# Two convolution blocks: pairs of units in the scan stage, inlaid convolution blocks at other places, and three steps in another order

## The chip, the cores and the metric

The kernel runs on one core of a Trainium2 chip. A core has five engines that work through queues of their own and meet only at semaphores: TensorE (PE, with its weight loads shown apart as PEld), VectorE (DVE), ScalarE (ACT), GpSimd (POOL) and SyncE (SP, which here only issues transfers). TensorE writes to eight banks of PSUM, each of 128 partitions by 512 float32 values; the other operands lie in SBUF. The metric is the device time of one execution in microseconds. It is the median of several executions, and lower is better.

## The reference

The input x has the shape (8, 96, 96, 192) in float32. Two blocks follow each other, each with a group norm before it and a residual around it:

```
x = x + L0(gn(x));  x = x + L1(gn(x))        # gn: 32 groups of 6 channels, over the whole image

L0: proj  = gn(x) @ W_in + b_in              # 192 -> 384 channels
    local = depthwise 3x3 conv(proj)
    mixed = 0.25*(lr + rl + tb + bt) + local # four running means s = 0.6*s + 0.4*x: along w
                                             # forward and backward, along h forward and backward
    out   = layernorm(mixed) @ W_out + b_out # 384 -> 192

L1: y   = depthwise 7x7 conv(gn(x)) + bias
    y   = layernorm(y) @ w0 + b0             # 192 -> 768
    out = (gelu(y) @ w1 + b1) * gamma        # 768 -> 192
```

## The kernel before

The kernel has five stages in a row, with DRAM tensors between them. Nearly all of it stands in manual schedules: each engine works in the order in which the Python code emits its instructions, and a planner has no part in it. Pools of buffers add waits where a buffer comes round again.

**Stage A** (to about 756 us) computes the statistics of the first group norm and `proj`, which it stores by channel in `P_d`.

**Stage B** (to about 1793 us) is the stage of the scans. Of the 384 channels it takes four at a time, 96 blocks `k`, each as `NI` = 3 units `i`; one unit holds 128 rows (four sets of 32 values of w) by 2 x 4 images x 96 values of h. The loop (L779 to L827) runs over n = 3k + i, 291 passes, of which the last three only mix. One pass of it emits

- `conv_b` (L681): 24 products from `band` and `pin` into two PSUM tiles `pl` (pool `ps_l`, four banks), on TensorE as tiles of 34 rows by 32 columns. Each float32 product appears as two records, so a unit is 48 records at L688. Two ACT copies take the result into `loc` (L697), two more take the rows of one channel into `last` (L700).
- `scan_down` on VectorE (L721, along h downward), with a small POOL operation on its ends (L725), and `scan_up` of the unit before (L730).
- up to two store issues of finished results on POOL (L744).
- `mix_b` (L703) of the unit three passes earlier: eight products (16 records, L709 and L712, 128 or 96 rows by 32 columns) do the scans along w as a product with the matrices `mix` and `down`. They go into two PSUM tiles `pa` (pool `ps_a`, two banks), and ACT copies each to `mo` (L713).
- `add` (L775) on POOL, which adds z to `mo`.

On TensorE this gives convolution, mix, convolution, mix. Inputs `pin` and `band` are loaded through SP three blocks ahead.

**Stage C** (to about 2580 us) runs over 192 units u: TensorE turns and projects a column (`turn_c`, `project_c`, L1135 and L1141) into `pos` banks (pool `ps_o`, four banks, two for each unit), ACT sums squares (`square_c`, L1162), and in the next pass `scale_c` makes `ve` on VectorE (L1168) and `rs` on POOL (L1170), and `finish_c` on VectorE (L1175) scales and adds the residual into `x1c`, which frees the banks. `steps` holds lists of `bn_stats`, three at a time, which collect the statistics of the second group norm; after the first half of the images it also holds the five steps of `norm_c` (L980), each as a list of one: means, squares, powers, shift, spread. Two of them, squares and powers, begin with a product (`total`, L992) that stands in TensorE's queue behind the unit of the pass; powers and shift pass through a power on POOL (L1020). A pass takes its list from `steps` ahead of `finish_c`.

**Stage D** (to about 2902 us) is the first part of the 7x7 convolution. There are 32 blocks n (2 halves of the images x 16 sets of 12 channels); it does n = 0 to `N1` - 1 = 18. A block has 24 scalings of `raw` to `xin` (`scale_steps`, in three tiles t of eight, L958 on ACT for some n, L960 on VectorE) and a copy of `band` (`spread`, L964), then six `conv_d` (L1323): 12 products each (24 records at L1337, 63 rows by 64 columns) into two PSUM banks, and two ACT operations into `yo` (L1347). `bank` hands out the eight banks in a ring. `store_d` stores `yo` through SP. The results are loaded again as tiles `ya` and `yb` by `load_y`: `y_0` is tile 0, `y_1` tile 1, whose pieces go to SP or POOL; the last eight pieces of a tile (L1404) are on POOL. The layer norm of a unit of stage E is a chain of seven steps (`norm_steps_e`): sums, mean, center (VectorE), square (ACT, L1501), squares (VectorE), powers (POOL, L1513), scale (VectorE). The chain of the first two units runs during the last two blocks, n = 17 and 18: sums, mean, center of unit 0 ahead of block 17, and after the third `conv_d` of block 18 square, squares and powers of unit 0, sums, mean and center of unit 1, and scale of unit 0. The loads of `y_1` come at the end of block 17.

**Stage E** runs over 72 units u (a tile of y has two). A unit has a first layer in 3 parts for u < 36 and 2 parts later (`first_layer`: products of 128 rows, L1549, then of 64 rows, L1559; a gelu on ACT, L1568), and four `second_layer` of the unit before (L1579), with `xo` on VectorE (L1590) and a store on POOL (L1598). `turn_in` transposes the unit to come (L1534). Into the first units the 13 blocks left of the 7x7 convolution are laid: `slots` holds for each block three lists of scalings (on ACT) and six `conv_d` (in the pool `ps_y`, two banks), and `slot()`, called five times in a unit, takes the next list whatever it is. The five places are after the first part of the first layer and after each of the four second layers.

## Time and profile before

| what | value |
|---|---|
| time, median of 3 runs | 5424.39 us (5416.11 to 5430.3) |
| the profiled execution | 5428.47 us, its span 5426.5 us |
| granted clock of TensorE, mean | 0.986 |
| PE, DVE, ACT, POOL busy | 97%, 64%, 48%, 44% |
| stage A, 0 to 756: PE busy | 706.8 us |
| stage B, 756 to 1793: PE busy | 1029.1 of 1037 us |
| stage C, 1793 to 2580: PE busy | 765.3 of 787 us |
| stage D, 2580 to 2902: PE busy | 258.4 of 322 us, DMA share 0.97 |
| joint of D and E, 2902 to 2975: PE busy | 46.1 of 73 us |
| stage E with inlaid blocks, 2975 to 3880: PE busy | 901.2 of 905 us |
| stage E, rest: PE busy | 1540.7 of 1546 us |

The profile is that of one execution. A line in order of time has the start in us from the span's start, the duration of the group, the engine, the line of the code, the operation, what it writes and reads, the shape of the tile in TensorE's array (34*32 is 34 rows by 32 columns), the size and the number of records, and in brackets how long the engine was idle before it and what ended that. Records of a group may overlap, so the distance from start to start says more than the duration.

### The profile page before, as it was taken

The numbers are of one execution on the slowest core, as the hardware profiler recorded it, in microseconds if no ns is written. First come the engines' busy times: TensorE is split into PE (matmuls) and PEld (weight loads), VectorE is DVE, ScalarE is ACT, GpSimd is POOL, SyncE is SP. The second block draws the span as 40 slices with busy tenths as digits, with TensorE's granted clock in tenths as the row PEclk, the third lists the DMA queues.
The fourth block names the chain that finished last, engine by engine and source line by source line (L and its number), as shares of the span: only waits on it lengthen the run. The fifth ranks groups of instructions, "written<-read, shape, count | busy, mean of one in ns | idle before, by whom it ended". The sixth has DMA issues, their size and how long they took to land. (4 is left out here: it accounts for less than half of the span.)

```text
span 5426.5 us, 107918 instructions
## 1 busy us (share of the span) xinstructions
PE 5247.6 (97%) x42206; PEld 3346.3 (62%) x42206; DVE 3455.9 (64%) x6722; ACT 2581.9 (48%) x5765; POOL 2405.4 (44%) x2129
## 2 busy tenths in 40 slices
PE   6999999999999999999787999999999999999999
PEld 4666643333333799999454666666666666666667
DVE  6555539999999555555556555555566666566654
ACT  2444447777777566565434444454433333323232
POOL 1111128888888555555335222233233333333332
PEclk9999989999999999999898999999999999999999
DMA  7999869999999799899998455545433233332331
GB/s 221 285 286 277 251 183 239 247 240 244 246 243 246 230 306 308 273 301 312 282 308 206 119 137 135 131 120 138 108 79 78 80 81 85 87 92 80 81 78 41
DMA packets 784651, 1015.33 MB, mean 187 GB/s; under 512 B 322359, under 2 KB 658432, under 8 KB 782096
## 3 DMA queue, kind: packets, MB, share of 16 engines
q1 hardware_dynamic: 671432, 633.30, 44.3%
q0 software_dynamic: 86896, 336.90, 18.9%
q10 hardware_dynamic: 25816, 38.25, 3.1%
q8 instruction: 334, 5.47, 0.4%
q14 instruction: 173, 1.42, 0.1%
HBM read 603.70 MB, written 420.03 MB: 189 GB/s over the span
## 5 line engine op out<-in xcount | busy, mean ns | idle before, releaser
L1579 PEld LDWEIGHTS hp<-w1g,g 128*128 128x128 f32 x6912 | 1117.9, 190 | 140.7 <-issue 78.3
L1579 PE MATMUL hp<-w1g,g 128*128 128x192 f32 x6912 | 1174.9, 329 | 0.0
L1568 ACT ACTIVATE g<-hp,b0g 128x512 f32<-128x512 f32 x864 | 519.8, 693 | 1214.8 <-PE hp L1559 1191.9
L1598 POOL DMA_DIRECT2D out_dram<-xo x288 | 211.6, 735 | 1536.8 <-DVE xo L1590 1496.9
L1590 DVE TENSOR_TENSOR xo<-hp,r 128x384 f32<-128x384 f32 x288 | 229.0, 795 | 1002.2 <-PE hp L1579 998.7
L1549 PE MATMUL hp<-yT,w0w 128*128 128x512 f32 x1728 | 779.2, 597 | 22.1 <-DVE yT L1534 21.9
L1141 PE MATMUL po<-wc,mt 128*128 128x193 f32 x3456 | 667.4, 329 | 7.4 <-DVE x1c L1175 7.3
L688 PE MATMUL pl<-pin,band 34*32 34x380 f32 (+1 forms) x13824 | 636.6, 494 | 9.6 <-DMA pin<-PL_d 4.0
L775 POOL TENSOR_TENSOR mo<-mo,z 128x768 f32<-128x768 f32 x285 | 594.6, 2086 | 4.8 <-ACT mo L713 0.6
L1141 PEld LDWEIGHTS po<-wc,mt 128*128 128x128 f32 x3456 | 556.8, 192 | 9.0 <-DVE x1c L1175 8.6
L1549 PEld LDWEIGHTS hp<-yT,w0w 128*128 128x128 f32 x1728 | 321.2, 190 | 382.3 <-issue 350.5
L721 DVE TENSOR_TENSOR_SCAN z<-decay,loc 128x768 f32<-128x768 f32 x288 | 505.9, 1757 | 61.6 <-ACT loc L697 33.0
L730 DVE TENSOR_TENSOR_SCAN z<-decay,z 128x768 f32<-128x768 f32 x288 | 498.4, 1731 | 0.1
L1337 PE MATMUL hp<-xin,band 63*64 63x372 f32 (+1 forms) x4608 | 412.7, 496 | 70.9 <-ACT yo L1347 26.9
L688 PEld LDWEIGHTS pl<-pin,band 34*32 34x32 f32 x13824 | 234.4, 108 | 393.4 <-issue 386.7
L709 PE MATMUL pa<-loc,mix 128*32 128x384 f32 x3456 | 436.5, 498 | 0.0
L712 PE MATMUL pa<-last,down 96*32 96x384 f32 x1152 | 431.4, 498 | 1.0 <-ACT mo L713 1.0
L1559 PE MATMUL hp<-yT,w0w 64*128 64x512 f32 x1728 | 419.5, 611 | 0.0
L1513 POOL TENSOR_TENSOR rs<-tot,neg_half 32x32 f32<-32x32 f32 x72 | 395.6, 5494 | 46.1 <-DVE tot L1511 45.3
L1347 ACT ACTIVATE yo<-hp,dwb 128x384 f32<-128x384 f32 x384 | 197.1, 585 | 423.4 <-PE hp L1337 290.2
L697 ACT COPY loc<-pl 128x384 f32<-128x384 f32 x576 | 248.2, 483 | 312.3 <-PE pl L688 312.3
L395 PE MATMUL pm<-xT,win 128*128 128x384 f32 x1152 | 392.2, 491 | 0.0
(159 smaller groups left out, 7276.0 us busy)
## 6 DMA issues: line engine op xcount, KB each, us to landing
P<-po POOLq DMA_DIRECT2D x96, 1152.0 KB, 9.7
pin<-P SPq DMA_DIRECT2D x190, 576.0 KB
mt<-M SPq DMA_DIRECT2D x192, 384.0 KB
xq<-in_x_dram SPq DMA_DIRECT2D x96, 576.0 KB
xr<-in_x_dram SPq DMA_DIRECT2D x192, 288.0 KB
X<-x1c SPq DMA_DIRECT2D x144, 384.0 KB
out_dram<-xo POOLq DMA_DIRECT2D x288, 192.0 KB, 2.4
r<-X SPq DMA_DIRECT2D x35, 1536.0 KB
```

Of the source, the lines that this page charges most:

```text
L688: nc.tensor.matmul(pls[g][at * RB : (at + 1) * RB, :, lo:hi], band[rows, c, kh, :], pin[rows, c, :, NJ - 1 - j, lo + kh - 1 : hi + kh - 1] ...
L709: nc.tensor.matmul(pa[at], mix[:, i, at], loc[:, q], start=True, stop=True)
L712: nc.tensor.matmul(pa[at], down[:, to], last[:, q], start=True, stop=True)
L721: nc.vector.tensor_tensor_scan(zf, decay_f, loc.rearrange("p q n -> p (q n)"), 0.0, ALU.mult, ALU.add)
L730: nc.vector.tensor_tensor_scan(zr, decay_f, zr, 0.0, ALU.mult, ALU.add)
L775: eng.tensor_tensor(m, m, z, ALU.add)
L1141: nc.tensor.matmul(po, mt[:, m, j * 128 : (j + 1) * 128], wc[:, m], start=(m == 0), stop=(m == NC - 1),)
L1337: nc.tensor.matmul(pys[g][k * 64 : (k + 1) * 64, :, lo:hi], band[rows, k * GS + c, d * ZS : d * ZS + 64], xin[rows, :, :, k * GS + c, lo + ...
L1549: nc.tensor.matmul(hps[m, q], w0w[:, 0, m * 128 : (m + 1) * 128], yT[:, 2 * q], start=True, stop=False,)
L1559: nc.tensor.matmul(hps[m, q], w0w[p, 1, m * 128 : (m + 1) * 128], yT[p, 1], start=False, stop=True,)
L1568: nc.scalar.activation(g[:, m, q], hps[m, q], AF.Gelu, bias=b0g[:, m : m + 1], scale=1.0)
L1579: nc.tensor.matmul(po[:, q], g[:, m, q, k * 128 : (k + 1) * 128], w1g[:, m], start=(m == 0), stop=(m == NE - 1),)
```

## The change

In stage B the pass is cut into `begin_b` (the convolution's products), `local_b` (copy to `loc`, both scans), `keep_b` (copy to `last`) and `mixed_b` (stores, mix, add), and the loop takes two passes at a time. TensorE's order is then convolution n, convolution n + 1, mix n, mix n + 1. The order on ACT, VectorE and POOL stays: `loc`, `last`, `mo` of one pass, then of the next.

In stage C a list of a single step (those of `norm_c`) is run after `finish_c` of the pass, not before.

In stage D the third tile of block 18 is scaled on ACT, between the evictions of block 17; the copy of `band` and the first steps of unit 0's chain move up on VectorE accordingly. In block 18 the steps that stood after the third `conv_d` stand ahead of the first. The last eight pieces of `y_1` are issued after block 18, so behind the power of unit 0 on POOL. The `raw` loads of block 19 come after the load of `r` on POOL's queue.

In stage E each slot has a kind, `rows` or `conv`, and a place takes only its kinds: conv behind each of the three parts of the first layer, rows behind the second layers, both at the third second layer. The first layer has three parts as long as there are slots. In all 65 of the 78 inlaid `conv_d` stand between the 64-row products of the first layer and a second layer (15 before), 13 between a second and a first layer (63 between a second layer and a first or second layer before), and the first layer is cut into three parts in 28 units (36 before).

```diff
+            def local():
+                loc = wp.tile([128, NG, GB * S], F32, tag="loc", name="loc")
...
+            def keep():
+                at = slice(i * RB, (i + 1) * RB)
...
+            return local, keep
...
-                    locs[k, i] = conv_b(band, pin, i, lasts[k])
+                    halves[n] = conv_b(*now_b, i, lasts[k])
+            def local_b(n):
...
+                    locs[k, i] = halves[n][0]()
                     z = zs[k, i] = scan_down(locs[k, i])
...
-                if up_next is not None:
-                    scan_up(up_next)
-                up_next = z
+                if ups:
+                    scan_up(ups.pop(0))
+                if z is not None:
+                    ups.append(z)
+            def mixed_b(n):
...
+            for n in range(0, n_b, 2):
+                begin_b(n)
+                local_b(n)
+                keep_b(n)
+                if n + 1 < n_b:
+                    begin_b(n + 1)
+                    mixed_b(n)
+                    local_b(n + 1)
+                    keep_b(n + 1)
+                    mixed_b(n + 1)
+                else:
+                    mixed_b(n)
...
-            if n == 1 or n >= N1:
+            if n == 1 or n >= N1 or (n == N1 - 1 and t == NT - 1):
                 nc.scalar.activation(to, of, AF.Identity, bias=sh, scale=sc)
...
-                if steps:
-                    for step in steps.pop(0):
+                now = steps.pop(0) if steps else []
+                if len(now) > 1:
+                    for step in now:
                         step()
                 if held is not None:
                     ...
+                if len(now) == 1:
+                    now[0]()
...
-                NI + 1: y_1,
+                NI + 1: y_1[:-8],
...
                 if n == NI + 1:
                     chain = norm_steps_e(0)
-                    steps += chain[:3]
+                    per_t = len(steps) // NT
+                    between = steps[-1 - per_t : -1]
+                    steps = steps[: -1 - per_t] + steps[-1:] + chain[:3]
                     chain = chain[3:]
                 elif n == NI + 2:
                     nxt = norm_steps_e(1)
-                    between = chain[:3] + nxt[:3] + chain[3:]
-                    last = nxt[3:4]
+                    steps = chain[:3] + nxt[:3] + chain[3:]
+                    last = y_1[-8:] + nxt[3:4]
...
-                    if c == 2:
-                        for step in between:
-                            step()
+                    for step in between[2 * c : 2 * c + 2]:
+                        step()
...
-            for t in range(NT - 1):
-                load_raw(N1, t)
...
-        load_raw(N1, NT - 1)
...
         load_r(0, nc.gpsimd)
+        for t in range(NT):
+            load_raw(N1, t)
...
-            early_half = u < n_u // 2
-            parts, pool = (3, ps_h) if early_half else (2, None)
+            inlaid = bool(slots)
+            parts, pool = (3, ps_h) if inlaid else (2, None)
...
             first_layer(u, 0, parts, pool)
             chain.pop(0)()
-            slot()
+            slot("conv")
...
-            slot()
-            if early_half:
+            slot("rows")
+            if inlaid:
                 first_layer(u, 1, parts, pool)
+                slot("conv")
...
-            slot()
+            slot("rows", "conv")
...
-            if early_half:
+            if inlaid:
                 first_layer(u, 2, parts, pool)
+                slot("conv")
```

## The prediction

> **What bounds the kernel now.** I read the page first (TensorE busy 97%), then busy time by stage, because an average over stages with different limits says little; then the order of time inside the stretches that the change touches.
>
> The busy time of each engine in four stretches (span of the stretch, then busy time and instructions of PE, weight load, DVE, ACT, POOL; granted clock, DMA share, GB/s):
>
> ```profile
> 1300.00:1500.00 200.00, 200.00 (x3656) 69.13 (x3648) 193.93 (x115) 141.94 (x342) 175.04 (x190) 1.00 0.92 241
> 2240.00:2280.00 40.00, 32.69 (x200) 31.14 (x199) 15.72 (x46) 17.42 (x63) 20.89 (x16) 0.91 0.60 182
> 2900.00:2950.00 50.00, 27.95 (x102) 11.44 (x95) 39.62 (x87) 21.67 (x30) 20.87 (x14) 0.80 0.79 199
> 3200.00:3400.00 200.00, 200.00 (x1112) 123.79 (x1110) 102.90 (x213) 96.47 (x170) 61.33 (x30) 1.00 0.53 132
> ```
>
> Stage B (first row) has TensorE full, VectorE at 97% and the DMA engines at 92%: a gain on TensorE may run into one of them. The second row (the statistics inside stage C) and the third (from D to E) have holes in TensorE; the fourth, E with conv blocks in it, has none.
>
> One unit of stage B, in order of time (start, duration):
>
> ```profile
> 1400.32 2.15 PE L688 MATMUL pl<-pin,band 34*32 34x384 f32 x48
> ...
> 1402.40 0.52 PE L709 MATMUL pa<-loc,mix 128*32 128x384 f32 x2
> ...
> 1402.56 0.86 ACT L697 COPY loc<-pl 128x384 f32<-128x384 f32 x2 [0.89 <-PE pl L688]
> ...
> 1403.45 1.76 DVE L721 TENSOR_TENSOR_SCAN z<-decay,loc 128x768 f32<-128x768 f32 x1
> ...
> 1403.83 2.15 PE L688 MATMUL pl<-pin,band 34*32 34x384 f32 x48
> ```
>
> Convolution to mix 2.08 us, mix to the next convolution 1.43: the period is 3.51. A VectorE scan begins just as the copy of loc ends (1402.56 + 0.86), so TensorE sets the pace.
>
> **Part 1, two units at a time.** TensorE's order C M C M becomes C C M M; ACT, DVE and POOL keep their order. What goes is one pair of changes between array shapes (34x32 and 128x32) in two units. Six rounds of the convolution come to 6 x 0.3175 = 1.905 (at the start of B four convolutions run with no mix between, at half clock, and their loc copies start 3.81 apart: 1.905 at full clock) and four rounds of the mix to 1.27; 3.51 less 3.175 leaves 0.335 for a pair of changes. [...] Here two mixes now follow each other with two `pa` banks, which ACT must empty. The trace of before has such mixes, the last three of the stage:
>
> ```profile
> 1794.46 0.51 PE L712 MATMUL pa<-last,down 96*32 96x384 f32 x1 [0.95 <-ACT mo L713]
> ...
> 1795.38 0.48 ACT L713 COPY mo<-pa 128x384 f32<-128x384 f32 x1 [0.59 <-PE pa L709]
> ...
> 1795.91 0.51 PE L712 MATMUL pa<-last,down 96*32 96x384 f32 x1
> ```
>
> Start to start 1.45 (the next again 1.46), not 1.27: the second mix waits for the copy of the first, which ends at 1795.86. So a pair is 1.92 (C to C) + 2.08 (C to M) + 1.455 (M to M) + 1.43 (M to C) = 6.885, against 7.02: 0.135 saved. Regular units run from 816 to 1791 us: 975 / 3.51 = 278, 139 pairs, **19 us**; by the drain rule alone 47. The first six units end in a wait for input (789.6) that swallows their gain; nothing for them.
>
> Do the others keep up at 3.44? DVE: the second scan starts 1.67 to 1.68 after the first (1403.45 to 1405.12), 1.73 at most after the other: 3.34 to 3.41. The loc copies now come 3.8 and 3.1 apart, as loc(n+1) stands on ACT behind the copies of mix(n); six buffers let DVE run late by that 0.4. POOL is busy 3.07 a unit; the ends of scan n are fixed there more than 2 us before the upward scan needs them. The DMA share rises to 0.94. Bounds: 0 (one of them takes it all) to 47.
>
> **Part 2, the statistics behind finish_c** (stage C):
>
> ```profile
> 2249.00 1.82 PE L1141 MATMUL po<-wc,mt 128*128 128x193 f32 x6 [3.32 <-DVE x1c L1175]
> ...
> 2262.26 1.44 PE L1141 MATMUL po<-wc,mt 128*128 128x193 f32 x6 [2.26 <-DVE x1c L1175]
> ```
>
> DVE waits in a statistics step for a product queued behind a whole unit, with finish_c behind it, and TensorE then lacks a bank: 7.3 us with two more waits of 0.73 and 0.99, and some 3.7 more at half clock (200 instructions in 40 us where neighbouring stretches have 276: 11.0 in all). After: finish_c goes first. What is late next is the following unit's `ve`: in the squares step by gm to the reduction, 2.7 us, of which a unit of 3.9 hides all but 0.6. In the powers step POOL's power (5.44) still stands before `rs`: total to the freed bank stays 7.87 (2254.39 to 2262.26), less a unit of 3.9, 0.3 for the total and 0.4 of transposes leaves 3.2. So 7.3 becomes 3.8: **3.5 us**; the half clock may go or come with the 3.2 (bounds 0 and 8).
>
> **Part 3, from D to E.** In time, POOL's issues and TensorE's two long waits:
>
> ```profile
> 2909.05 2.28 POOL L1404 DMA_DIRECT2D yb<-Y  x4 [17.67 <-DMA yb<-Y]
> 2911.40 6.21 POOL L1513 TENSOR_TENSOR rs<-tot,neg_half 32x32 f32<-32x32 f32 x1
> ```
>
> ```profile
> 2922.37 5.23 PE L1549 MATMUL hp<-yT,w0w 128*128 128x512 f32 x8 [20.35 <-DVE yT L1534]
> ...
> 2970.67 4.04 PE L1337 MATMUL hp<-xin,band 63*64 63x384 f32 x24 [4.86 <-DVE band L964]
> ```
>
> The first power is ready at 2905.6 but sits behind four loads of `yb`, which wait. Ahead of it lie sums (bound by the landing of yb at 2890.3, not moved), center (ends 2896.4), ACT's square. After: square goes before block 18's evictions (2896.4 to 2899.4; before it ended at 2902.2), the DVE reduction and totals take 3.3 (2902.7), the power runs at once (to 2909) beside unit 1's sums to center (7.9 on DVE, to 2910.6), and the scale with transposes takes the same 4.73 to the first product: 2915.3, **7.1 us** sooner. What moves besides: block 18's evictions start 3 us later on ACT, and its last two convolutions wait for banks to about 2904, under the hole; eight scales of 0.45 go from DVE to ACT between evictions, where it idles 0.84 before each pair; y_1's eight POOL issues (0.57 each) now stand behind the power and land by about 2918, where sums of unit 2 want them at 2920.5 (a miss costs 2 to 3); six raw loads (0.62 each) go behind the 1.2 us issue of r on POOL's queue, so r lands earlier than 2947.9, and with it bias, the next power and DVE's band copy, which the second wait is for. The first conv slot also comes one product later. I take the **4.9** as gone: 12 us (bounds 2 and 18).
>
> **Part 4, conv blocks behind half-height products.**
>
> ```profile
> 3222.71 4.17 PE L1579 MATMUL hp<-w1g,g 128*128 128x192 f32 x24
> 3226.81 2.13 PE L1337 MATMUL hp<-xin,band 63*64 63x384 f32 x24
> 3228.86 3.70 PE L1549 MATMUL hp<-yT,w0w 128*128 128x512 f32 x8
> 3232.50 1.99 PE L1559 MATMUL hp<-yT,w0w 64*128 64x512 f32 x8
> 3234.41 2.13 PE L1337 MATMUL hp<-xin,band 63*64 63x384 f32 x24
> 3236.47 4.17 PE L1579 MATMUL hp<-w1g,g 128*128 128x192 f32 x24
> ```
>
> Between second and first layer a block costs 4.10 + 2.05 + 3.64 = 9.79, where without it the two take 4.00 + 3.53 (3245.92, 3253.82 and 3257.35 start such a run: 7.90 is two second layers): 2.26. Behind the half-height product (1.91 + 2.06 + 4.00 against 1.92 + 4.00) it costs 2.05. In the order of instructions 15 of 78 blocks stand so before and 65 after: 50 x 0.205 = 10.2 us. Eight units go from three parts to two: three are 3 x 5.45, two are 2 x 8.02 (5.24 + 2.78 at 4306), and one second layer less pays 0.10 behind a half-height product: 0.41 each, 3.3. The blocks' waits for scales (2.9 on ACT, 0.8 on band) mostly go, as the block now comes a product later: 2. Together **15.5** (bounds 8 and 18). The two banks of a block are emptied by ACT in 1.05 us, hidden under 3.9 of second layer.
>
> **Sum.** 19 + 3.5 + 12 + 15.5 = 50. The profiled execution took 5428.5 (span 5426.5, 2 around it), so it would take 5378.5; from the median of the runs, 5424.4, 5374.
>
> **Rivals.**
> (a) Stage B gains nearly nothing: POOL or DVE turns into the bound, or ACT comes late to `pa`. For: DVE 97%, POOL 87%, `pa` tight. Against: DVE and POOL fit as worked out, and ACT is free 0.9 us before the first mix ends. 31 to 36 us remain: 5391.
> (b) The banks don't bind and the full change of shape is saved, 47 for 19: 5346. Against: the three last mixes.
> (c) Slower: DVE can't run late. If each scan waited for the copy before it and for POOL's fix of the ends, a unit of B would take more than two whole scans (1.76 + 1.73 = 3.49). It decides from 31 / 278 = 0.11 over the present 3.51, so from 3.62; at 3.7 the kernel takes 5424 + 53 - 31 = 5446. Against: scans overlap by 0.08 in the trace and nothing but loc holds them.
> (d) The reordering changes no time at the joints (parts 2 and 3 at their low ends, 2): 5387.
>
> **How the numbers follow.** A measurement here tells about 0.3%, 16 us. Forecast 0.56, (a) 0.17, (b) 0.10, (d) 0.09, (c) 0.04, and 0.04 for partial losses that cancel the gain. The likeliest case's own range is 5360 to 5390; with (a), (b) and (d) 5344 to 5400. Faster: 0.56 + 0.17 + 0.10 + 0.09 = 0.92; same 0.04; slower 0.04.
>
> **What would show it.** Right: in B, convolutions in groups of 96 records, a period of 6.88 per pair with the second mix about 1.45 after the first; in C waits of under 1 and about 3 us; the first layer's first product 13 us, not 20, after the last conv block; blocks followed by the second layer; TensorE full in E. Wrong: pairs near 7.0 with DVE waiting for loc or near 6.7 (then the banks were misjudged); a conv block that waits on ACT in E; sums waiting for y_1.

## The result and the profile after

The changed kernel took 5403.56 us (median of 20 executions, 5372.46 to 5421.39) beside 5412.75 us for the kernel before on the same chip (20 executions, 5401.91 to 5430.30). The ratio of the two, 0.9973 with a 95% interval of 0.9962 to 0.9985, stands for some 15 us (the medians alone differ by 9). Forecast were 5374 us and a range of 5344 to 5400, worked out from a median of 5424.4 of three executions, so the change gained less than a third of the 50 us. The profiled execution of after is its fastest (5372.46, span 5370.6), that of before is near its longest (5428.47): the two profiles differ by 56 us, more than the sum of the prediction, and the repeated timings do not. That gap is what the experiments below are about.

Busy time by stage of after (columns as in the prediction: PE, weight load, DVE, ACT, POOL, each with its instructions; then granted clock, DMA share, GB/s), for stage B, the statistics in C, the joint, and E with blocks:

```profile
1300.00:1500.00 200.00, 200.00 (x3720) 71.47 (x3708) 193.96 (x117) 144.78 (x348) 177.01 (x193) 1.00 0.95 247
2190.00:2230.00 40.00, 39.40 (x271) 38.26 (x269) 22.24 (x61) 24.46 (x89) 24.14 (x19) 1.00 0.94 298
2870.00:2920.00 50.00, 38.56 (x124) 18.85 (x125) 40.31 (x80) 22.55 (x38) 29.36 (x25) 0.86 0.83 222
3170.00:3370.00 200.00, 198.57 (x1117) 125.43 (x1116) 109.63 (x222) 88.53 (x150) 57.20 (x30) 1.00 0.45 115
```

B issues 3720 products in 200 us where before had 3656, at a DMA share of 0.95 for 0.92. In E TensorE is no longer quite full. One pair of units of B in order of time:

```profile
1395.90 4.07 PE L688 MATMUL pl<-pin,band 34*32 34x384 f32 x96
...
1399.91 0.52 PE L715 MATMUL pa<-loc,mix 128*32 128x384 f32 x3
...
1401.37 0.82 PE L715 MATMUL pa<-loc,mix 128*32 128x384 f32 x3
...
1402.79 3.44 PE L688 MATMUL pl<-pin,band 34*32 34x384 f32 x80
```

Both convolutions take 4.01 to the first mix, the second mix starts 1.46 after the first, the next pair 1.42 later: 6.89, against 6.885 in the prediction, and the median of 131 pairs is 6.88. Where nothing disturbs it, the pair does what was forecast.

The joint in after, all engines (start, duration; the bracket is the idle time before and what ended it):

```profile
2892.17 5.42 POOL L1469 TENSOR_TENSOR r<-r,b1g 128x3072 f32<-128x3072 f32 x1 [6.26 <-DMA r<-X]
2892.77 5.91 DVE L1518 TENSOR_TENSOR ya<-ya,m 128x1024 f32<-128x1024 f32 x1
...
2892.99 1.10 PE L1588 MATMUL hp<-yT,w0w 128*128 128x512 f32 x2 [0.96 <-DVE yT L1573]
2898.60 1.21 DVE L1518 TENSOR_TENSOR yb<-yb,m 128x1024 f32<-128x1024 f32 x1
...
2900.91 2.05 PE L1588 MATMUL hp<-yT,w0w 128*128 128x512 f32 x2 [6.83 <-DVE yT L1573]
```

VectorE's centering of unit 2 (`ya<-ya,m`), 1.23 us elsewhere, takes 5.91, as long as GpSimd adds the bias to `r` beside it; the transposes of unit 1 stand behind it, and TensorE waits 6.83 us for them. The first product of the first layer did come earlier, after a wait of 8.97 us instead of 20.35.

Blocks of E in after:

```profile
3239.73 1.99 PE L1598 MATMUL hp<-yT,w0w 64*128 64x512 f32 x8
3242.34 2.13 PE L1376 MATMUL hp<-xin,band 63*64 63x384 f32 x24 [0.62 <-ACT xin L994]
3244.39 4.17 PE L1618 MATMUL hp<-w1g,g 128*128 128x192 f32 x24
3248.40 3.60 PE L1588 MATMUL hp<-yT,w0w 128*128 128x512 f32 x8
3251.93 1.99 PE L1598 MATMUL hp<-yT,w0w 64*128 64x512 f32 x8
3253.84 2.13 PE L1376 MATMUL hp<-xin,band 63*64 63x384 f32 x24
3255.90 4.17 PE L1618 MATMUL hp<-w1g,g 128*128 128x192 f32 x24
```

The second of these blocks costs 2.06 (3253.84 to 3255.90), as forecast; the first, which is the first of its tile, waits for its scales.

### The profile page after: what moved, and what is told of

It reads as the page before. It is cut to its first block, busy times and chain, and to the rows that moved or that the text cites. A ratio compares the mean times of both kernels' runs of the same rounds, so it can differ in the third digit from the quotient of the medians.

```text
span 5370.6 us, 107820 instructions
## 1 busy us (share of the span) xinstructions
PE 5210.4 (97%) x42206; PEld 3351.1 (62%) x42206; DVE 3454.0 (64%) x6714; ACT 2584.0 (48%) x5773; POOL 2411.8 (45%) x2129
## 3 DMA queue, kind: packets, MB, share of 16 engines
q8 instruction: 334, 5.47, 0.5%
q14 instruction: 173, 1.42, 0.1%
## 4 chain that ended last, share of the span: by engine, by line
PE 85%; DMA 5%; issue 3%; DVE 2%; SPq 2%; ACT 1%; POOL 1%; ACTq 0%; POOLq 0%; DVEq 0%
PE hp L1618 19%; PE hp L1588 12%; PE pl L688 11%; PE po L1177 10%; PE hp L1598 7%; PE pm L395 6%; PE pa L715 5%; PE hp L1376 4%; PE pt L1171 3%; DMA Y<-yo 3%; PE pm L408 3%; PE pa L718 3%; PE pt L381 2%; ACT xin L994 1%; SPq L1247 1%
## 5 line engine op out<-in xcount | busy, mean ns | idle before, releaser
L688 PE MATMUL pl<-pin,band 34*32 34x380 f32 (+1 forms) x13824 | 603.9, 490 | 6.6 <-DMA pin<-PL_d 4.1
L688 PEld LDWEIGHTS pl<-pin,band 34*32 34x32 f32 x13824 | 255.3, 108 | 346.0 <-issue 333.0
L1376 PEld LDWEIGHTS hp<-xin,band 63*64 63x64 f32 x4608 | 212.7, 138 | 266.9 <-issue 137.9
L719 ACT COPY mo<-pa 128x384 f32<-128x384 f32 x576 | 261.4, 480 | 177.4 <-PE pa L715 175.1
```

The lines of the kernel that those rows point to most:

```text
L688: nc.tensor.matmul(pls[g][at * RB : (at + 1) * RB, :, lo:hi], band[rows, c, kh, :], pin[rows, c, :, NJ - 1 - j, lo + kh - 1 : hi + kh - 1] ...
L1376: nc.tensor.matmul(pys[g][k * 64 : (k + 1) * 64, :, lo:hi], band[rows, k * GS + c, d * ZS : d * ZS + 64], xin[rows, :, :, k * GS + c, lo + ...
```

## The experiments

Eighteen kernels ran. The table gives each one's time against the kernel before (timed beside it on the same chip) and the length of the stages in its one profiled execution: B from its first convolution to C's first transposition, C to D's first product, D to the first product of 64 rows in the first layer (the 5 to 6 us of products of 128 rows before it count as D), E the rest. The light, heavy, shifted and padded ones do other work in B; the text says which.

```
                                   ratio [95%]              B       C      D       E
before                             1                      1045.1  791.0  335.4  2499.0
after                              0.9973 [.9962,.9985]   1020.5  780.5  321.9  2491.7
e1 pairs alone                     1.0007 [.9995,1.0019]  1035.9  789.5  325.0  2494.4
e2 inlaid blocks alone             0.9991 [.9983,1.0000]  1036.8  790.2  330.6  2484.2
e3 statistics and joint alone      0.9981 [.9971,.9992]   1038.3  785.8  325.0  2493.6
e4 whole change again              0.9977 [.9966,.9987]   1045.2  788.8  320.1  2492.2
e5 pairs, half the pin loads       0.9959 [.9945,.9974]   1019.3  791.9  329.0  2492.2
e6 no pairs, half the pin loads    0.9993 [.9982,1.0003]  1033.0  785.8  327.9  2493.0
e7 no pairs, more loads            1.0020 [1.0009,1.0030] 1044.8  787.9  331.1  2495.8
e8 change without pairs            0.9964 [.9947,.9981]   1034.2  784.2  321.2  2491.7
e9 pairs, loads spread             1.0005 [.9994,1.0016]  1028.7  794.6  329.7  2491.9
e10 e8, transposes first           0.9964 [.9951,.9977]   1042.2  782.9  321.3  2490.6
e11 e10 and empty slot             0.9966 [.9954,.9978]   1053.9  782.8  324.0  2484.4
e12 e11, pairs, loads spread       0.9967 [.9955,.9980]   1039.1  783.2  317.1  2485.0
e13 pairs, shifted                 1.0123 [1.0097,1.0149] 1027.1  785.9  327.8  2493.4
e14 e11, square behind gelus       0.9949 [.9933,.9965]   1042.6  788.8  322.4  2478.5
e15 pairs, padded                  1.0587 [1.0565,1.0609] 1245.2  787.3  330.9  2492.4
e16 e14, pairs, padded             1.0530 [1.0509,1.0552] 1235.9  786.8  320.2  2478.9
e17 pairs, small pads              0.9998 [.9985,1.0010]  1034.2  795.8  329.5  2497.1
e18 e14, pairs, small pads         0.9949 [.9929,.9969]   1032.3  784.3  325.8  2477.6
```

**The parts.** The first four kernels (e1 to e4) are hunks of the change's own diff and the whole of it again. They were expected at 0.9954, or 0.998 to 1.000 if later stages give the gain back (e1), at 0.9971 or 0.9987 (e2), at 0.9971 or, if the joints vary by execution, 0.998 to 1.000 (e3), and near 0.9973 (e4). The pairs alone bring nothing: 1.0007 is outside both forecasts, and no later stage is longer. C with the statistics moved averages 784.8 us over ten profiles, 790.0 over ten without: 5.2 us, give or take 1.4. D with the joint reordered averages 321.9 over ten and 329.7 over ten: 7.8 us, give or take 1.2. E gains 10.2 with the inlaid blocks alone (2494.4, the mean of the nine kernels with neither of the two parts, to 2484.2), 0.8 with the joint alone, and only 2.5 with both (2491.9, mean of after, e4 and e8): so joint and blocks together give back some 8 us in E that each alone did not. (The nine scatter from 2491.9 to 2499.0, so differences of 2 or 3 us in one profile say little.)

**Where the pairs' gain goes.** B's length in the table also holds its start, and that varies for reasons of its own: in every kernel without pads the granted clock is 0.50 for 27 to 68 us of B's first 110, pairs or not (48 in before, 34 in after, 68 in e11, whose TensorE was busy 46.00 of the 46 us from 790 to 836). So the stretch from the start of unit 24 to that of unit 286 (counted from 0; 131 pairs) is the better measure. It takes 919.6 to 922.2 us in all seven kernels without pairs at normal load, and 907.8 in after. Of the 24.6 us by which the profile of after is shorter in B, 13.1 lie there and the rest is the start.

In e4 the pairs lose what they gain in one stretch of B (busy time by 100 us, columns as above):

```profile
1100.00:1200.00 100.00, 99.41 (x1827) 36.33 (x1814) 95.03 (x57) 70.78 (x170) 85.95 (x95) 1.00 0.93 238
1200.00:1300.00 100.00, 97.80 (x1692) 35.04 (x1688) 89.88 (x54) 66.58 (x160) 81.36 (x89) 0.97 0.87 233
1300.00:1400.00 100.00, 95.65 (x1672) 33.74 (x1664) 87.79 (x54) 65.63 (x159) 80.25 (x88) 0.97 0.85 220
1400.00:1500.00 100.00, 100.00 (x1892) 36.02 (x1888) 97.45 (x59) 73.14 (x176) 88.81 (x98) 1.00 0.94 249
```

After issued 1849 and 1876 products in the two middle stretches, e4 1692 and 1672: 361 fewer, 19.5 us at 18.5 products a microsecond. In order of time, TensorE stands in the middle of a convolution, and no semaphore is named as the cause ("issue"):

```profile
1266.35 0.86 PE L688 MATMUL pl<-pin,band 34*32 34x384 f32 x13
1268.94 5.53 PE L688 MATMUL pl<-pin,band 34*32 34x384 f32 x83 [1.73 <-issue]
1274.40 0.85 PE L715 MATMUL pa<-loc,mix 128*32 128x384 f32 x2
```

After the stop, 83 products take 5.53 us; by the 4.07 for 96 at a granted clock of 1.00 (after, at 1395.90) they would take some 3.5. The granted clock was 0.50 for 6.8 us from 1271 on, and the pair with this stop is 5.7 us longer than the median pair.

What was late are, by their count and their places, TensorE's instructions. The page lists a DMA queue q8 of kind "instruction", 334 packets and 5.47 MB: 16 KB each. 334 packets of 256 instructions make 85,504, and the trace has 84,412 matmuls and weight loads of TensorE and some 1,200 of its semaphore instructions (85,610 records in after, 256.3 for each packet). The places of the stops agree: if all these records are counted from the start of the trace, every one of the 57 stops of over 0.8 us in the regular part of B that stand on "issue", in ten kernels, comes at a count that leaves the remainder 193 when divided by 256, so whole packets apart, at the first instruction of one. (The only other stop, a wait for pin in e7, leaves 132.) In B a packet is used up in 6.9 us (137 of them from 820 to 1765 us in after), and at full load it lands only 3 to 4 us (median; 3.6 in before, 3.3 in after) before its first instruction. The packets around the stop in e4, and the data packets of the hardware queue that loads pin:

```
q8 packets (start - end):  1249.09-1250.14   1254.05-1255.41   1266.62-1267.72   1270.87-1271.83
burst of pin packets:      1259.15 to 1267.05, with the stores beside it 15 to 16 DMA engines busy
TensorE goes on at:        1268.94
```

The packet came 12.6 us after the one before, just as the burst ended, and TensorE went on 1.2 us after its end. So it was at every stop listed below: the restart came 1.2 to 1.6 us after the end of an instruction packet, the last that had landed. The seven profiles at normal load without pairs (before, e2, e3, e8, e10, e11, e14) have no such stop.

First test, the load. For every odd channel group from the fifth on, e5 and e6 skip the pin loads and read the tile of the group before (so half of the convolutions use other data); e5 with pairs, e6 without:

```diff
         def load_b(k):
-            for g in range(NG):
-                load_pin_b(k, g)
+            if k % 2 and k >= 5:
+                tiles_b[k] = tiles_b[k - 1]
+            else:
+                for g in range(NG):
+                    load_pin_b(k, g)
```

> The pairs of stage B alone, with the loads of pin left out for every odd channel group from the fifth on (its units read the tile of the group before: the output is another one, the instructions of every engine but SP are the same). Theory 'late code': in the run of the pairs alone TensorE stood still in mid-convolution with nothing awaited, after TensorE's instruction packets (queue q8) had come over 11 us apart behind data packets. With the load nearly halved no gap between these packets is over 11 us, TensorE never stands, stage B takes 1017 to 1022 us in every execution, and against the same light load without pairs the kernel is 14 to 20 us faster. Rival 'engines': VectorE, GpSimd or ACT now and then can't follow a pair of 6.88 us; then halving the DMA load changes nothing, B stays at 1035 to 1045 in some executions and the gain against the unpaired light kernel is 0 to 6 us, as it was at full load.

> The kernel before with the same loads of pin left out. Theory 'late code': without pairs the load makes little difference, since fetches were on time already: stage B 1036 to 1038 us, the whole within 4 us of the kernel before. Rival 'the DMA bounds B even without pairs': B falls clearly, by more than 5 us.

From 0.9993 to 0.9959: the pairs gain 0.34%, 18 us, in the time, and 17.0 us in the 131 pairs (921.0 to 904.0; 0.135 a pair would be 17.7). Busy time from 1200 to 1400 us, of e5 and then of e6 (columns as above):

```profile
1200.00:1400.00 200.00, 200.00 (x3716) 72.25 (x3712) 194.14 (x117) 145.22 (x349) 178.73 (x193) 1.00 0.64 187
```

```profile
1200.00:1400.00 200.00, 200.00 (x3652) 69.14 (x3648) 194.01 (x114) 141.82 (x343) 174.20 (x190) 1.00 0.63 180
```

VectorE, ACT and GpSimd do the same work per unit as at full load and follow the pairs without trouble, so the rival "engines" is out: it is the DMA traffic that takes the gain. Not as forecast: gaps of over 11 us between packets still occur (five, up to 11.84), only without a stop. The gap alone does not make one: e8, without pairs, has six.

Second test, more load without pairs (the same stretch is compared with e8's): e7 loads three more rows of each pin tile into rows that nothing reads.

```diff
             part(RB + 1, RB + 2)
+            if k >= 3:
+                nc.sync.dma_start(
+                    pin[p + 40 : p + 43].rearrange("p c b j h -> p c (b j h)"),
+                    P_d[g][m][c, 0:3].rearrange("c r b j h -> r c (b j h)"),
+                )
```

> The kernel before (no pairs) with three more rows of each pin tile loaded into rows that nothing reads: 216 KB more per channel group, some 8 % of stage B's traffic, so that the DMA share rises from 0.92 to about 0.97 to 0.98. Theory 'late code': TensorE stands in mid-convolution for want of instructions here too, without any pair: gaps of over 11 us between instruction packets, waits put down to 'issue', stage B 10 to 40 us longer. Rival 'it belongs to pairs' (their order of instructions, not the load): no such stalls, B within 3 us of 1037 unless a convolution waits for pin itself.

A miss, and a test of something else than meant: the traffic rose to 252 GB/s from 243, but the DMA share fell to 0.86 from 0.91. Packets came earlier, not later (4.55 us ahead by the median, for 3.5 to 3.9 in the seven), and TensorE stood once, 4.5 us for pin itself, and one pair was 7.9 us longer (the kernel is 1.0020, 11 us slower). More bytes alone don't make packets late. Whether busier DMA engines would, without pairs, no run tells.

Third, the bursts. e9 issues the two pin tiles and the bands of a group at its three units instead of all at the first:

```diff
                         elif k + 3 < n_k:
-                            loads.append(load_b(k + 3))
+                            load_pin_b(k + 3, 0)
+                            bands_b[k + 3] = tile_band_b(k + 3)
+                            loads.append((bands_b[k + 3], tiles_b[k + 3]))
+                    elif i == 1 and 0 < k < n_k - 3:
+                        load_pin_b(k + 3, 1)
+                    elif i == 2 and 0 < k < n_k - 3:
+                        load_band_b(k + 3)
```

> The pairs of stage B alone at full load, but the loads of a channel group (two pin tiles of 576 KB and the bands) issued one by one at the group's three units and not all at its first. Theory 'late code behind bursts': TensorE's instruction packets come late because they wait behind 1.2 MB queued at once; spread out, none is late enough to stop TensorE, B is 1018 to 1023 us, ratio to before 0.9960 to 0.9975. Theory 'late code by the load itself', wherever it is queued: as with the pairs alone, 0.999 to 1.002, with TensorE standing 1 to 2 us at a time in some executions.

The time is that of the pairs alone, and TensorE still stopped five times (0.9 to 1.2 us). So spreading does not help. That it makes the stops shorter one profile doesn't show, since after, unspread, has only two, of 0.8 and 0.9.

Fourth, the place. A pair takes a little more than 256 instructions of TensorE, so the start of a packet moves backward through it, four product records (of 128) in about 21 us. The stops, as time (gap between two starts) at record, in two runs of the pairs:

```
e1   1222.87 (0.86) at 21   1265.86 (1.96) at 13   1310.34 (2.23) at 5   1332.19 (1.21) at 1   1688.15 (1.18) at 59
e4   1182.61 (0.81) at 29   1204.43 (0.85) at 25   1268.94 (2.21) at 13   1316.78 (2.15) at 5   1342.42 (1.84) at 1   1364.47 (1.84) at 125
```

The longest come in the same stretch of B, 1260 to 1365 us, at the same records. Is it the place or the time? e13 and e15 put products ahead of a convolution that overwrites them, to move the start of the packets: e13 64 ahead of the first unit, e15 100 ahead of it and 72 ahead of units 92 and 180.

```diff
+            for _ in range(pad):
+                nc.tensor.matmul(
+                    pls[0][:RB], band[: RB + 2, 0, 1, :], pin[: RB + 2, 0, :, 0, :],
+                    start=True, stop=True,
+                )
```

> The pairs of stage B alone, with 64 matmuls (128 instructions with their weight loads) put ahead of the first convolution, whose result is overwritten. In the runs with pairs TensorE always stopped at the instruction where a 256-instruction packet begins; that place moves backward through the pair, from record 59 of 128 at 1009 us to 13 at 1266, 1 at 1337 and 121 at 1375, and the long stops (1.2 to 2.5 us) came while it was between 29 and 121 (through 0), at 1176 to 1375 us, every third packet, each when a burst of pin packets began just before the packet was due. Theory 'alignment': with 128 instructions more the same places are reached elsewhere: stops at 820 to 1030 and 1480 to 1730 us, none between 1130 and 1340, and the record at which each stops follows the old one less 64. Rival 'the data in that stretch' (what the DMA does at 1176 to 1375 us, whatever TensorE's alignment): the stops stay at 1170 to 1380 us. Time about that of the pairs alone, 0.999 to 1.002.

> The pairs of stage B alone, with overwritten matmuls that keep the start of an instruction packet away from the first convolution of a pair: 100 ahead of the first unit, 72 ahead of units 92 and 180 (3 us each at full clock). Theory 'alignment': the start of a packet goes from record 120 to 63 three times and never through 0, so TensorE never stops over 1 us; B takes 1025 to 1030 us, about 7 us more than undisturbed pairs, in every execution; ratio to before 0.9965 to 0.9985. Rival (alignment doesn't set it): stops as before plus 6 to 9 us of added work, ratio 1.001 to 1.003.

Both were missized. Such a product is two records and two weight loads, four instructions, and its records came 0.63 us apart at a granted clock of 0.50 (in e15 the first 200 took 126.4 us), where 48 records of a convolution, 0.49 us each, take 2.15 us together at 1.00. In e13 the 64 products were 128 records (79 us) and 256 instructions: a whole packet, which moves nothing. In e15 the 488 records cost some 320 us, and put the start of the packets at record 17 at the outset. So the times say nothing, but the stops do (those of over 1.5 us):

```
e15   988.57 (1.82) at 17   1078.93 (2.09) at 1   1105.54 (1.52) at 125   1128.44 (2.25) at 121
     1623.61 (1.51) at 29   1764.66 (1.63) at 5   1813.38 (2.38) at 125   1835.75 (1.72) at 121
```

With B beginning 125 us later than in e4, the records 17 to 121 now come at 988 to 1128, where e4 would be at 863 to 1003 and had no stop; there the stops are, and again at 1764 to 1836, after the last pads had put the start back to 7. They go with the place of the packet's start. e17 puts in small products (8 columns), 48 ahead of the first unit and 21 ahead of unit 134, to keep the start away from records 0 to 29:

> The pairs of stage B alone, again with overwritten matmuls, now of 8 columns and rightly counted (each is two records and two weight loads, four instructions: the 64 of the shifted run were 256 instructions, a whole packet, and moved nothing; those of the padded run put the packets' starts at record 17 at the outset, in the bad range). 48 ahead of the first unit put the start of a packet at record 124 of 128, and 21 ahead of unit 134, where it has come to 38, put it back to 124: it stays between 124 and 30 by the long way round, never in 0 to 29 for long. Theory 'alignment': no stop of TensorE over 1.2 us but for the last 50 us of the stage, B 1020 to 1027 us, ratio to before 0.9960 to 0.9980. Rival: stops of 1.2 to 2.5 us come all the same; ratio 0.999 to 1.002.

The count was off again: in the trace the start is at record 7 behind the first pads (781 us), where 124 was meant, and at 8 behind the second (1245 us), so it passes the bad places twice. The first time, from 781 to 908 us, there is one stop, of 0.95; the second time two of 2.46 and 2.32 us, at records 127 and 123 (1289 and 1312 us). The time is 0.9998: no better than without pads. So the place is not enough: the same records come with and without a stop (after, too, passes them from 1200 to 1365 us without one). Whether an alignment that avoids all bad places would keep the gain, no run here tells.

What all late packets cost together can be read off the pairs. The median pair takes 6.88 us in every kernel with pairs, at any load, against 7.02 for two units without. The gain of 18 us is lost again in single pairs that are longer:

```
                                 131 pairs, us    lost in pairs over 0.25 us    packets that land less than
                                                  above the median, us          1.75 us ahead, of 132
seven without pairs              919.6 to 922.2    0.0 to 2.5                    0 to 10
e6 no pairs, half the pin loads  921.0             1.3                           4 (of 131)
e5 pairs, half the pin loads     904.0             2.1                           9
after                            907.8             5.7                          23
e9 pairs, loads spread           911.9             9.8                          25
e1 pairs alone                   919.0            16.3                          31
e12                              926.7            24.2                          32
e4 whole change again            928.0            26.0                          30
```

The last column counts the packets that end less than 1.75 us before their first instruction, so with nothing to spare. Each of the lengthened pairs in this table holds such a packet. The losses, 5.7 to 26.0, average 16.4 us at full load: that is the gain.

**The joint.** Is it GpSimd's bias? e8 is the change without pairs, and in e10 VectorE's transposes of unit 1 go ahead of the centering of unit 2 that stood:

```diff
             second_layer(u - 1, 1, pool)
-            chain.pop(0)()
+            if u:
+                chain.pop(0)()
...
             turn_in(u + 1, 1)
+            if u == 0:
+                chain.pop(0)()
```

> The changed kernel without the pairs of stage B (statistics behind finish_c, joint from D to E and inlaid blocks kept). If the pairs bring nothing on average because their gain is eaten by late code, this is as fast as the whole change: ratio to before 0.996 to 0.998 (the two halves alone measured 0.9991 and 0.9981), with a narrower spread of its times. If the pairs do bring part of their 17 us, it is 0.1 to 0.3 % slower than the whole change, 0.998 to 1.000. In E the conv blocks should wait as in the run of the inlaid blocks alone, and unit 1's yT should come 5 to 7 us late as in the whole change, because the GpSimd addition of the bias to r then runs beside VectorE's centering of unit 2.

> The change without pairs, with one edit at the start of E: in unit 0, VectorE's centering of unit 2 is put behind the transposes of unit 1 instead of before them. Theory 'lock': the second half of the centering (two inputs in SBUF) stood 4.7 us because GpSimd's addition of the bias to r ran, and the transposes behind it made TensorE wait 7 us for unit 1's yT. With the transposes first that wait falls to under 1.5 us, E takes 2484 to 2487 us for 2491.7, the centering itself is still stretched to about 6 us if it meets the addition, and the kernel is 0.1 % faster than the change without pairs. Rival 'only the order on VectorE': unit 1's data are late for another reason (the power, the landing of y_1); then TensorE still waits 4 us or more for them.

e8 is as fast as the whole change. In e10 the wait for the transposes is gone and another takes its place (all engines in order of time):

```profile
2913.22 5.43 POOL L1433 TENSOR_TENSOR r<-r,b1g 128x3072 f32<-128x3072 f32 x1 [6.77 <-DMA r<-X]
...
2915.20 4.53 DVE L1482 TENSOR_TENSOR ya<-ya,m 128x1024 f32<-128x1024 f32 x1
...
2919.65 1.21 DVE L1482 TENSOR_TENSOR yb<-yb,m 128x1024 f32<-128x1024 f32 x1
2919.81 1.97 ACT L1504 ACTIVATE sq<-ya 128x1024 f32<-128x1024 f32 x1 [9.65 <-issue]
...
2923.16 1.22 PE L1552 MATMUL hp<-yT,w0w 128*128 128x512 f32 x1 [7.13 <-ACT g L1571]
```

The centering ends again just after GpSimd's addition; ACT's square of it stands ahead of the gelus that free TensorE's banks. In the rows of this case, of centering and addition the one that began first took its usual time and the other was stretched. Where the addition came first the centering takes 4.53 (e10) and 5.91 (after) for 1.23, ending 1.1 us behind the addition's end; in e3, where the centering came first, its halves take 1.18 and 1.21 and the addition 6.49 for 5.42. In the traces of before and after 61 of the 72 additions begin 0.04 to 0.06 us behind the centering of `yb`, which takes 1.21 to 1.23, and the additions 6.45 to 6.47; in the last unit of after, where both begin at 5275.31, the addition takes 5.45 and the centering 6.53. VectorE's transposes take 1.00 us beside the addition (2913.32 and 2914.26 in e10), for 1.05 by the median of after. e14 (with the empty slot below) also puts the square of unit 2 behind the last gelus of unit 0:

```diff
             turn_in(u + 1, 1)
-            chain.pop(0)()
+            if u:
+                chain.pop(0)()
...
                 slot("conv")
+            if u == 0:
+                chain.pop(0)()
```

> The change without pairs, with the empty slot and the transposes first, and in unit 0 ACT's square of unit 2 put behind the last gelus of unit 0. Theory 'lock': in the run with the transposes first, the wait moved from the transposes to ACT, where the square stood behind the blocked centering and the gelus behind the square (7.1 us). With the square behind the gelus nothing on TensorE's path waits for the blocked centering: no wait over 1.5 us in unit 0, E 2477 to 2480 us for 2484.4 and 2485.0, ratio to before 0.9945 to 0.996. Rival: the next in the chain (the power of unit 2, the bank of unit 0's results) takes its place and E stays at 2483 or more.

E falls to 2478.5 (again 2478.9 and 2477.6 in e16 and e18), 6.3 us under e11 and e12. TensorE's waits in e14 from 2880 to 4100 (total, times, longest):

```profile
PE hp L1552 <- DVE yT L1537: 9.0, 1, 9.0
PE hp L1340 <- ACT yo L1350: 2.4, 1, 2.4
PE hp L1552 <- ACT g L1571: 2.4, 2, 1.6
```

The 9.0 is the wait for the first product, which stays. That settles the joint: the gain was handed to an addition which had moved under the centering (in e14 the centering still takes 6.24 beside it, but nothing of TensorE's stands behind it).

**The first block of each tile.** TensorE's waits in after over the same part:

```profile
PE hp L1588 <- DVE yT L1573: 7.8, 2, 6.8
PE hp L1376 <- ACT xin L994: 6.0, 8, 0.9
PE hp L1376 <- DVE band L1000: 2.5, 4, 0.6
```

e11 leaves an empty slot between a tile's last scales and its first block:

```diff
                 ("rows", scales[2 * per_t :]),
+                ("conv", []),
             ]
```

> The run before with an empty slot between the last scales of a tile and its first conv block. Theory: the first block of each of 13 tiles waits 0.6 to 1.1 us for scales (ACT) or the band copy (VectorE), and runs 0.4 longer at half clock behind it, since the block's place came directly behind the slot with these steps. With the empty slot these waits go: 10 to 14 us less, against 1 to 2 us for three or four more units in three parts. E 2473 to 2478 us, ratio to before 0.993 to 0.9955. Rival: the waits are filled anyway or the blocks wait for something else next (banks, the next tile's raw loads): E stays within 3 us of the run before.

The twelve waits for `xin` and `band` are gone, and E falls by 6.2 (2490.6 to 2484.4; I had expected 10 to 14, and had read a half clock into the blocks behind these waits: the one at 3164.20 in after takes 2.55 us for 2.13, but the granted clock there is 1.00), of which 2.6 belong to a wait for `yo` at the joint that happened to be shorter (4.2 to 1.6). The time does not show it: 0.9966 after 0.9964, with intervals some 14 us wide.

**All together.** e12 is e11 with the pairs and the spread loads, e16 and e18 are e14 with the pairs and the pads of e15 and e17.

> The whole change with the three edits: loads spread over the units, transposes first in unit 0, an empty slot ahead of each tile's first block. If spreading the loads lets the pairs keep their gain: ratio to before 0.990 to 0.9925 (0.3 % under the run without pairs). If not: the same as without pairs, 0.993 to 0.9955.

> The whole change with transposes first, square behind the gelus, the empty slot, and the added matmuls of the run before. If they let the pairs keep about 10 us: 0.993 to 0.9945, under the same without pairs by 0.1 to 0.2 %. If not, 0.996 or more.

> The whole change with transposes first, the square behind the gelus, an empty slot ahead of each tile's first block, and the small added matmuls. If the pairs keep 10 us or more of their 17: ratio to before 0.9920 to 0.9935, below the same without pairs (0.9949). If they don't: 0.994 to 0.996.

e12 equals e11 (0.9967 and 0.9966, both above what was forecast), e18 equals e14 (0.9949 both): once more the pairs add nothing. e16 pays for its pads. The best version is the change without pairs, with the three small edits (e14): 0.9949, 28 us under before, and nearly twice the gain of the change as it is. Its interval still overlaps that of e8 (0.9964), so what the three edits are worth rests on the length of E in three profiles.

## Why the prediction was wrong

Of the 50 us, 35 did not come. 19 of them are part 1, and 18 lie in stage E (15.5 and 4.9 forecast, 2.5 measured); C and D gave 2 more than forecast.

**Part 1, the step that failed:** "0.135 saved" a pair, times "139 pairs", 19 us; the timings of the pairs alone (1.0007, 1.0005, 0.9998) show nothing saved within some 6 us. The period was right (6.88): the two `pa` banks bind (1.46 start to start; in after the weight loads of the mixes wait 154 us in all for ACT's `mo`, from 820 to 1765). The "drain rule" behind the 47 is shown by no run: the 47 is 139 times the 0.335 that the prediction estimated for a pair of changes of shape, and what the runs showed in its place is 0.14 saved in a pair (6.88 for 7.02). What failed is that the period was taken to hold for every pair. "The DMA share rises to 0.94" stands in the prediction and was given no price; TensorE's own instructions come over these DMA engines (q8, 1.1% of their time in B of after), and with pairs 21 to 32 of 132 packets landed with nothing to spare, which lengthened single pairs by 5.7 to 26 us in sum. With half the loads 17 of the 17.7 us are there (e5 against e6). Rival (a) held in what it said of B, that it gains nearly nothing, but not in its reason, which was GpSimd, VectorE or ACT (e5 rules these out), and not in its total of 5391, which took E's gain as safe. Rivals (b) and (c) are out by the period; (d) by C and D.

What stays open: why packets land with nothing to spare so much more often with pairs (21 to 32 times, 0 to 10 without), although a pair needs its code only 2% sooner; and why the number of late ones differs so much from execution to execution. That the one profile of after lost least to them at full load (5.7 us), and that the one of before had a long start of B at half clock, was luck: it made the sum look fulfilled.

**Part 2** was right: 3.5 forecast, 5.2 measured. The waits of the statistics in after, total 3.9 us for 7.3 before (two, the longer 3.5), are the "3.8" of the prediction, and the half clock is gone (1.00 in that row).

**Part 3** was right in its first half: the first product was to come 7.1 us sooner, and D is 7.8 us shorter. The second half, the 4.9 taken as gone, failed: without any change to it that wait is 2.5 and 2.2 us in e1 and e9, so the profile of before had shown a large one, and E gained 0.8 from part 3 alone, which is within the scatter. Worse, the prediction counted "r lands earlier than 2947.9, and with it bias" as help. In after the addition ran at 2892.2, 0.6 us before the centering of unit 2; it was priced as a step of GpSimd's queue, and never set against what VectorE does beside it. TensorE waited 6.8 us behind it. In e3 it came 1.1 us after the start of that centering's first half, and the wait for unit 1 was 1.7 us. So it hangs on when `r` lands.

**Part 4** was right in its main term: 2.05 a block. The 2 us of waits for scales that were to "mostly go" had the wrong sign: a block behind the half-height product comes directly behind the place that holds its last scale, and twelve waits of 0.6 to 0.9 us stand in after where e1 has five. E gained 10.2 in e2 for 15.5.

The sum, measured by stages: 5.2 (C) + 7.8 (D) + 2.5 (E) + 0 (B) = 15.5, and 0.9973 is 14.6.

## What to carry to other kernels

In a stage with TensorE full and the DMA engines busy to 0.90 to 0.95, a denser order of products did not pay here, although every engine could follow (at 0.64 it did): in such a stage look at the instruction queue's packets (q8 here), and test the change once with half the data loads before believing one profile. Compare such a stage over a stretch that leaves out its start: here the clock of the first 110 us alone moved its length by up to 20 us. When a step is brought forward, list what runs on the other engines at its new time, and above all whether a long GpSimd operation now begins just ahead of a VectorE operation that others wait for: here an addition of 5.42 us made a centering of 1.23 us take 4.5 to 6.5, and left transposes at 1.00. A product that is put right behind the step that feeds it wants one place of slack: twelve of them waited 0.6 to 0.9 us in after, none in e11.

## What the runs showed of the hardware

- The page of after lists 334 packets of 16 KB in a DMA queue of kind "instruction" (q8), for 85,610 records of TensorE, so one for each 256; in B they took 1.1% of the time of the 16 DMA engines, beside 92% for the data of q0 and q1. In B, which used one in 6.9 us, a packet landed 3 to 4 us before its first instruction at full load (median). All 57 stops of over 0.8 us on "issue" stand at the first instruction of such a packet, 1.2 to 1.7 us after it landed; the longest gap from start to start was 2.7 us.
- Behind some stops the clock was half: the granted clock was 0.50 for 6.8 us behind the two of 2.15 and 2.21 us in e4, and stayed at 1.00 behind those of 1.96 and 2.23 in e1.
- At the start of B it was 0.50 for 27 to 68 us, a different length in different executions (48 in before, 34 in after, 68 in e11), though TensorE was busy (46.00 of 46 us in e11).
- The place of a packet's start within B's repeating pair of about 256 instructions moved slowly (four product records in 21 us), and the longest stops came while it was at a few records of it, in three different stretches of time (e1 and e4 from 1266 to 1364 us, e15 from 989 to 1128 and from 1765 to 1836); the same records passed without a stop as well.
- VectorE's centering of 1.23 us (`ya<-ya,m`) took 4.5 to 6.5 beside one GpSimd addition of 5.4 us that had begun before it (after, e4, e8, e10, e11, e14); where the centering had begun 0.04 to 0.06 us before, it took 1.21 to 1.23 and the addition 6.45 to 6.47 (61 times in before and after).
- A product of 32 columns of weights, one of 100 alike in a row, took 0.63 us a record at a granted clock of 0.50 (e15); the same shape in a convolution of 48 records took 0.045 at 1.00 (before, 2.15 us for 48).
